# A graph network's edges ordered by source: the ordering's output written by plain DMAs to fixed rows instead of scatters

## The chip, the cores and the metric

The kernel runs on one core of one Trainium2 chip. The time is device microseconds of one execution, the median of three runs. A profile is one further execution, recorded instruction by instruction; its times below are counted from its first instruction. PE is TensorE, PEld its weight load, DVE VectorE, ACT ScalarE, POOL GpSimd, and SP SyncE, which only issues DMAs here.

## The reference

Two layers of a graph network over 20000 nodes of 256 features and 340000 edges, which come sorted by their destination `dst`:

```python
# layer 0: a relational convolution, applied twice, with relu between
xW  = einsum('ni,rio->rno', x, W)           # 8 relations
agg = segment_sum(xW[edge_type, src], dst)
h   = agg + x @ self_w + b
# x = layernorm(x + layer0)
# layer 1: attention with 4 heads, its sums taken by src
h   = (x @ W).reshape(n, 4, 64)
e   = leaky_relu(hl[src] + hr[dst]);  ee = exp(e - max over src)
out = segment_sum(ee / segment_sum(ee, src)[src] * h[dst], src)
# x = layernorm(x + layer1)
```

Layer 0 sums by destination, the order in which the edges arrive. The attention sums by source, so the edges must also be put into an order by source. This order is made on the chip, and the change is about it.

## The kernel before

Edges are taken 128 at a time, as columns of tiles with one edge on each partition: 2657 such columns ("tiles" of the rounds), 16 to a chunk, 166 chunks. Blocks are 128 nodes; there are NB = 157.

The program has four stages.

- **Start** (lines 270 to 492, driven from line 1706). `split_rows` reads x in 40 pieces and writes it as three bf16 parts to the table `xs`. Between the pieces, one step of `chunks` each prepares edge lists. After the second piece the class `ordered` (line 741) is set up and `fill_rows` writes padding rows.
- **Rounds one and two** (`round_one`, `round_two`, both through `by_chunks`, line 498). For each tile POOL gathers 128 rows of the table with an indirect DMA (`gather`, line 511), 20 tiles ahead of its use, into 24 buffers. PE multiplies the gathered parts with one-hot matrices (line 606), a chunk's sums are copied out (line 543, ACT and DVE), multiplied with the weights (line 562), and the result is written by SP. Round one writes `h2s`, which is the table of round two. Round two writes the rows of `table3s` for the attention.
- **Attention** (line 1114). For each block, 17 tiles gathered from `table3s` (line 1169) by lists loaded from `to3d`, `own3d` and `ownd`.

The order by source is made in the shadow of the rounds. `ordered.run` is a Python generator; each `yield` ends a *step*. `by_chunks` advances it with `next(side)` in those tiles for which `pace(u)` holds: in round one every tile up to number 905 and then three of four, in round two four of seven. What is left at the end of round two would run uncovered. The order of instructions on every engine is the program's order (a manual schedule), and each engine works in order, so an instruction that waits holds up what is behind it on its engine.

The generator's parts are:

- `count` (818): how many edges of each block are in each group of columns. The columns are dealt into G = 29 groups.
- `records` (793) and `places` (838): from the counts, for each group and block, the place of its first edge. A block has room for T3 = 17 columns of 128 edges, and one more that stays empty or takes an overflow; `col` is the column in which a group begins.
- `write` (895): for each group, one-hot products on PE put the edges of all blocks into place, one column for each block: a tile of 128 places by 157 blocks. What a group leaves of a column begun earlier is carried in `held`, so that a column which several groups fill is written by each of them, more complete each time. `finish` (971) transposes the tile (`turn`, 993, giving `t` with one block on each partition; two buffers) and, two steps later, `out_` (1003) writes it: for 128 and then for 29 blocks, one indirect DMA on POOL puts each block's row of 128 numbers at row `at` of `recs3`, which is block times 18 plus column. The last write to a row stands. After the last group a 30th write puts the carried rest into the next column.
- `unpack` (1062): 23 loads of 126 rows of `recs3` by SP; each is split into parts by DVE, transposed by PE, copied by ACT, and written to `ownd`, `to3d` and `own3d`.

`recs3` is set to zero at the start by 18 DMAs on ACT's queue (line 777). The scatters are lines 1006 to 1008, and `self.at` holds their row numbers, set in lines 889 to 892.

Of the kernel before, what the change touches and what calls it, by code (L numbers as in the profile page):

```python
# [34 lines left out]
F32 = mybir.dt.float32  # L35
BF16 = mybir.dt.bfloat16
I32 = mybir.dt.int32
# [3 lines left out]
ALU = mybir.AluOpType  # L41
AX = mybir.AxisListType
# [5 lines left out]
P = 128  # L48
# [8 lines left out]
T3 = 17  # L57
# [9 lines left out]
def gnn_kernel(  # L67
# [17 lines left out]
    nc = tc.nc  # L85
# [5 lines left out]
    NB = (N + P - 1) // P  # L91
# [22 lines left out]
    G = -(-COLS // GT)  # L114
# [25 lines left out]

    xp = dram.tile([NR, D], F32, name="xp")
    x1s = dram.tile([NR, D], F32, name="x1s")
    recs3 = dram.tile([NB * (T3 + 1), P], I32, name="recs3")

    ownd = dram.tile([NB * (T3 + 1), P], BF16, name="ownd")
    to3d = dram.tile([P, NB, T3 + 1], I32, name="to3d")
# [10 lines left out]
    iota = const.tile([P, P], F32, name="iota")  # L157
# [583 lines left out]
    class ordered:  # L741
# [6 lines left out]
        def __init__(self, keep, k):  # L748
            self.k = k

            self.pending = False
            self.base = keep.tile([P, 2], F32, name="base")
            nc.gpsimd.iota(self.base, pattern=[[P * (T3 + 1), 2]], base=0, channel_multiplier=T3 + 1,
                           allow_small_or_imprecise_dtypes=True)
            self.count_all = keep.tile([P, G, NB], FP16, name="count_all")
            self.place16 = keep.tile([P, NB], FP16, name="place16")
            self.cross16 = keep.tile([P, NB], FP16, name="cross16")
            self.at = keep.tile([P, 2, G + 1], I32, name="at")
            self.band = keep.tile([P, 2 * P - 1], FP16, name="band")
            nc.vector.memset(self.band, 0.0)  # L760
            nc.vector.memset(self.band[:, P - 1:P], 1.0)
            self.below = keep.tile([P, P], F32, name="below")
            nc.gpsimd.memset(self.below, 1.0)
            nc.gpsimd.affine_select(out=self.below, in_=self.below, compare_op=ALU.is_gt, fill=0.0, base=0,
                                    pattern=[[1, P]], channel_multiplier=-1)
            self.below16 = keep.tile([P, P], FP16, name="below16")
            nc.vector.tensor_copy(self.below16, self.below)
            self.ident16 = keep.tile([P, P], FP16, name="ident16")
            nc.vector.tensor_copy(self.ident16, ident)
            self.row = keep.tile([P, 1], F32, name="row")  # L770
            nc.gpsimd.iota(self.row, pattern=[[0, 1]], base=0, channel_multiplier=1,
                           allow_small_or_imprecise_dtypes=True)
            zero = keep.tile([P, NB], I32, name="zero")
            nc.vector.memset(zero, 0)
            flat = recs3.rearrange("t p -> (t p)").rearrange("(p c) -> p c", p=P)
            for c in range(T3 + 1):
                nc.scalar.dma_start(flat[:, c * NB:(c + 1) * NB], zero)

            self.lots = []
            for g in range(G):  # L780
                n = len(range(g, COLS, G))
                self.lots += [(g, i, min(LOT, n - i), n) for i in range(0, n, LOT)]
# [55 lines left out]
        def places(self, sp, ps):  # L838


            pc = ps.tile([P, 512], F32, name="pr")[:, :NB]
            for g in range(G):
                nc.tensor.matmul(pc, self.band[:, P - 1 - g:2 * P - 1 - g], self.count_all[:, g, :],
                                 start=(g == 0), stop=(g == G - 1))
            many = sp.tile([P, NB], F32, name="many", bufs=1)
            nc.scalar.copy(many, pc)
            yield
            yield
            pc = ps.tile([P, 512], F32, name="pr")[:, :NB]
            nc.tensor.matmul(pc, self.below, many, start=True, stop=True)  # L850
            begin = sp.tile([P, NB], F32, name="begin", bufs=1)
            nc.vector.tensor_copy(begin, pc)
            end = sp.tile([P, NB], F32, name="end", bufs=1)
            nc.vector.tensor_add(end, begin, many)

            over = sp.tile([P, 2, NB], F32, name="over", bufs=1)
            nc.vector.tensor_single_scalar(over[:, 0, :], many, float(P), op=ALU.is_gt)
            nc.vector.tensor_single_scalar(over[:, 1, :], end, float(T3 * P), op=ALU.is_gt)
            nc.vector.tensor_single_scalar(over[:, 1, NB - 1:], end[:, NB - 1:], float(tiles_of(NB - 1) * P), op=ALU.is_gt)
            overs = sp.tile([P, 1], F32, name="overs", bufs=1)  # L860
            nc.vector.tensor_reduce(overs, over.rearrange("p a b -> p (a b)"), op=ALU.add, axis=AX.X)
            yield
            yield
            po = ps.tile([P, 512], F32, name="pr")[:, :NB]
            nc.tensor.matmul(po[0:1, 0:1], ones[:, 0:1], overs, start=True, stop=True)
            nc.vector.tensor_add(bad, bad, po[0:1, 0:1])
            yield
            yield
            nc.vector.tensor_scalar_min(begin, begin, float(T3 * P))
            nc.vector.tensor_scalar_min(end, end, float(T3 * P))  # L870
            whole = sp.tile([P, NB], I32, name="whole", bufs=1)
            bits = sp.tile([P, NB], I32, name="bits", bufs=1)
            col = sp.tile([P, NB], F32, name="col", bufs=1)
            nc.vector.tensor_copy(whole, begin)
            nc.vector.tensor_single_scalar(bits, whole, P - 1, op=ALU.bitwise_and)
            nc.vector.tensor_copy(self.place16, bits)
            nc.vector.tensor_single_scalar(bits, whole, 7, op=ALU.arith_shift_right)
            nc.vector.tensor_copy(col, bits)
            nc.vector.tensor_copy(whole, end)
            nc.vector.tensor_single_scalar(bits, whole, 7, op=ALU.arith_shift_right)  # L880
            nc.vector.tensor_tensor(self.cross16, bits, col, op=ALU.subtract)
            nc.vector.memset(self.at, 0)
            yield
            yield
            for s in range(0, NB, P):
                n, x = min(P, NB - s), s // P
                pt = ps.tile([P, 512], F32, name="pr")
                nc.tensor.transpose(pt[:n, :P], col[:, s:s + n], ident)
                nc.vector.tensor_scalar(self.at[:n, x, :G], pt[:n, :G], self.base[:n, x:x + 1], None, op0=ALU.add)
                nxt = sp.tile([P, 1], F32, name="nxt", bufs=1)  # L890
                nc.vector.tensor_scalar(nxt[:n], pt[:n, G - 1:G], 1.0, float(T3), op0=ALU.add, op1=ALU.min)
                nc.vector.tensor_add(self.at[:n, x, G:], nxt[:n], self.base[:n, x:x + 1])
                yield

        def write(self, sp, ps, pi):
            k = self.k
# [74 lines left out]
            def finish(g, pl):  # L971
# [31 lines left out]
                def out_(c):  # L1003
                    for s in range(0, NB, P):
                        n = min(P, NB - s)
                        nc.gpsimd.indirect_dma_start(
                            out=recs3, out_offset=bass.IndirectOffsetOnAxis(ap=self.at[:n, s // P, c:c + 1], axis=0),
                            in_=v["t"][:n, s // P, :], in_offset=None)


                wait = [lambda: None] * 2
# [49 lines left out]

        def unpack(self, sp, ps):

            each = P // (T3 + 1)
            lots = [(b, min(each, NB - b)) for b in range(0, NB, each)]

            def load(b, n):
                r = sp.tile([P, 2, P], I32, name="t")[:, 0]
                nc.sync.dma_start(r[:n * (T3 + 1)], recs3[b * (T3 + 1):(b + n) * (T3 + 1), :])
                return r  # L1070

            r = load(*lots[0])
            yield
            for i, (b, n) in enumerate(lots):
                m = n * (T3 + 1)
                nxt = load(*lots[i + 1]) if i + 1 < len(lots) else None
                yield
                f = sp.tile([P, P], F32, name="uf", bufs=1)
                nc.vector.tensor_copy(f[:m], r[:m])
# [1 line left out]
                nc.vector.tensor_single_scalar(bits[:m], r[:m], P - 1, op=ALU.bitwise_and)  # L1081
                own = sp.tile([P, P], BF16, name="uo")
                nc.vector.tensor_copy(own[:m], bits[:m])
                nc.sync.dma_start(ownd[b * (T3 + 1):b * (T3 + 1) + m, :], own[:m])
                yield
                pt = ps.tile([P, 512], F32, name="pr")
                nc.tensor.transpose(pt[:, :m], f[:m], ident[:m, :m])
# [2 lines left out]
                yield  # L1090
                to = sp.tile([P, P], I32, name="ud", bufs=1)
                nc.vector.tensor_single_scalar(to[:, :m], t[:, :m], 7, op=ALU.arith_shift_right)
                nc.sync.dma_start(to3d[:, b:b + n].rearrange("p b t -> p (b t)"), to[:, :m])
                bits = sp.tile([P, P], I32, name="ub", bufs=1)
                nc.vector.tensor_single_scalar(bits[:, :m], t[:, :m], P - 1, op=ALU.bitwise_and)
                own = sp.tile([P, P], BF16, name="uo")
                nc.vector.tensor_copy(own[:, :m], bits[:, :m])
                nc.sync.dma_start(own3d[:, b:b + n].rearrange("p b t -> p (b t)"), own[:, :m])
                r = nxt

    def split(pool, v, shape, name):
# [640 lines left out]
```

## Time and profile before

| | us |
|---|---|
| median of 3 runs | 14361.06 (14348.96 to 14382.09) |
| the profiled execution | 10529.01 |
| its span, first to last instruction | 10527.3 |
| first gather of round one | 204 |
| last gather of round one, first of round two | 3612, 3635 |
| last gather of round two | 7037 |
| first scatter of the ordering, last | 1528, 6755 |
| loads of the unpacking, first and last | 6759, 6900 |
| attention's lists loaded | 7060 |

The profiled execution is 3832 us shorter than the median of the runs, and durations from the profile belong to it alone. Each stage has its own bound, so the busy share over the whole span says little; what counts is what an engine waited for within a stage. The mean granted TensorE clock was 0.968 of full speed.

### The profile page before, as it was taken

The page shows a single profiled execution, that of the slowest core. Times are in us where ns is not written, and L with a number is a line of the kernel's source. Part 1 is how long each engine was busy: PE and PEld are TensorE (multiplying, and loading weights), DVE is VectorE, ACT ScalarE, POOL GpSimd, SP SyncE. Part 2 cuts the span into 40 slices and gives each one's busy share as a digit, 9 for nine tenths or more (in the row PEclk, how much of TensorE's full clock was granted, in tenths as well). Part 3 has the DMA queues.
Part 4 walks back from the last instruction along what each step waited for, and adds up shares of the span by engine and source line. Part 5 has one row for each costly group of instructions (what it writes and reads, how often), then busy time and mean ns, then how long its engine had stood idle before and what let it go on. Part 6 is the DMA issues. An engine that isn't in the chain of part 4 may idle for free.

```text
span 10527.3 us, 226558 instructions
## 1 busy us (share of the span) xinstructions
PE 9180.0 (87%) x78961; PEld 7148.1 (68%) x78961; DVE 7514.2 (71%) x20993; ACT 5874.9 (56%) x19300; POOL 7717.9 (73%) x8094
## 2 busy tenths in 40 slices
PE   2999999999999899999999999887777777777777
PEld 2888888878888788888888888764444444444444
DVE  6666676666666666666666666438888888888888
ACT  3111145545545444444444444218888888888888
POOL 2777777777777677777777777767777777777776
PEclk6999999999999999999999999999999999999999
DMA  8666666656666566666666666665555555555554
GB/s 276 178 178 178 175 171 175 172 171 176 170 173 175 171 184 186 182 186 185 184 183 186 185 185 183 189 183 149 152 152 153 152 152 153 153 154 153 153 153 126
DMA packets 831294, 1815.05 MB, mean 172 GB/s; under 512 B 199083, under 2 KB 477820, under 8 KB 829988
## 3 DMA queue, kind: packets, MB, share of 16 engines
q0 software_dynamic: 472592, 1420.50, 49.0%
q1 hardware_dynamic: 348582, 371.97, 11.2%
q8 instruction: 620, 10.16, 0.4%
q10 hardware_dynamic: 8958, 7.99, 0.3%
q14 instruction: 542, 4.44, 0.1%
HBM read 1663.28 MB, written 136.59 MB: 171 GB/s over the span
## 4 chain that ended last, share of the span: by engine, by line
PE 52%; DVE 12%; POOL 11%; issue 10%; DMA 7%; ACT 7%; SPq 0%; ACTq 0%; DVEq 0%; POOLq 0%
PE pm L562 23%; PE a L606 15%; POOL g L1169 11%; DVE dump L1223 3%; DMA g<-table3s,to 3%; PE pl L964 3%; ACT g L1265 3%; DMA g<-xs,idx 2%; PE pm L558 2%; DVE b L788 2%; PE pr L925 1%; PE pr L728 1%; PE pr L926 1%; DMA g<-h2s,idx 1%; PE po L1279 1%
## 5 line engine op out<-in xcount | busy, mean ns | idle before, releaser
L511 POOL DMA_INDIRECT g<-xs,idx x2657 | 2525.3, 950 | 989.4 <-issue 368.3
L1169 POOL DMA_INDIRECT g<-table3s,to x2657 | 2597.9, 978 | 840.5 <-issue 775.0
L606 PE MATMUL a<-s,g 128*128 128x184 bf16 (+10 forms) x37860 | 2977.5, 223 | 204.8 <-DMA own<-xs 108.1
L511 POOL DMA_INDIRECT g<-h2s,idx x2657 | 2514.0, 946 | 826.6 <-issue 368.1
L606 PEld LDWEIGHTS <-g 128*128 128x128 bf16 x37860 | 2531.0, 98 | 549.0 <-issue 132.2
L562 PE MATMUL pm<-wt,to 128*128 128x256 f32 x10624 | 2887.7, 395 | 0.0
L1265 ACT ACTIVATE g<-g 128x64 f32<-128x64 f32 x9984 | 2435.4, 334 | 5.1
L562 PEld LDWEIGHTS pm<-wt,to 128*128 128x128 f32 x10624 | 1814.3, 191 | 177.5 <-issue 0.9
L1279 PE MATMUL po<-g,s 128*128 128x260 f32 x5314 | 1730.5, 417 | 79.7 <-DVE g L1271 50.6
L543 ACT COPY to<-a 128x512 f32<-128x512 f32 x996 | 545.5, 582 | 2242.5 <-PE a L606 2167.3
L1223 DVE CUSTOM_DVE_ANT_0 dump<-pr,pen 128x768 bf16<-128x768 f32 x1876 | 1616.6, 905 | 97.8 <-PE pr L1220 96.6
L946 DVE CUSTOM_DVE_ANT_0 dump<-pr,b 128x157 f16<-128x157 f32 x2657 | 712.3, 319 | 1105.0 <-PE pr L926 1099.0
L936 ACT ACTIVATE two<-b,hi 128x157 f16<-128x157 f16 x2657 | 1123.5, 423 | 319.7 <-DVE b L788 206.5
L1220 PE MATMUL pr<-hpt,pick 128*128 128x512 bf16 (+2 forms) x3752 | 930.5, 331 | 343.7 <-DVE top L1223 337.3
L788 DVE TENSOR_TENSOR b<-pi,kb 128x471 f16<-128x471 f32 (+1 forms) x1798 | 1109.8, 635 | 150.2 <-PE pr L830 77.5
L1279 PEld LDWEIGHTS po<-g,s 128*128 128x128 f32 x5314 | 852.2, 197 | 419.6 <-ACT g L1265 90.0
L937 ACT ACTIVATE two<-b,lo 128x157 f16<-128x157 f16 x2657 | 1101.3, 414 | 0.0
L522 DVE TENSOR_TENSOR s<-pi,code 128x1280 bf16<-128x1280 f32 (+1 forms) x666 | 1094.7, 1644 | 4.8 <-DMA xs<-s 4.8
L1220 PEld LDWEIGHTS <-pick 128*128 128x128 bf16 x3752 | 379.4, 101 | 832.8 <-issue 708.3
L1209 ACT CAST hpt<-pr 12x768 bf16<-12x768 f32 (+1 forms) x469 | 350.4, 747 | 358.9 <-PE pr L1207 358.6
L1207 PE MATMUL pr<-identb,g 128*12 128x128 bf16 x2657 | 267.2, 221 | 315.2 <-DMA g<-table3s,to 271.6
L964 PE MATMUL pl<-two,a 128*128 128x314 f16 x2657 | 509.3, 301 | 18.1 <-DVE a L952 17.2
(270 smaller groups left out, 9189.3 us busy)
## 6 DMA issues: line engine op xcount, KB each, us to landing
ob<-ownd SPq DMA_DIRECT2D x625, 128.0 KB
g<-xs,idx POOLq DMA_INDIRECT x2657
g<-h2s,idx POOLq DMA_INDIRECT x2657
g<-table3s,to POOLq DMA_INDIRECT x2657
own<-xs SPq DMA_DIRECT2D x166, 192.0 KB
h2s<-h SPq DMA_DIRECT2D x166, 192.0 KB
own<-h2s SPq DMA_DIRECT2D x166, 192.0 KB
xs<-s SPq DMA_DIRECT2D x39, 768.0 KB
```

Source lines behind the costliest of these rows:

```text
L511: nc.gpsimd.indirect_dma_start(out=g, out_offset=None, in_=table, in_offset=bass.IndirectOffsetOnAxis(ap=idx[:, u:u + 1], axis=0))
L522: nc.vector.tensor_tensor(s, pi[:, :w].unsqueeze(1).to_broadcast([P, e - f, w]), code[:, c:c + e - f].unsqueeze(2).to_broadcast([P, e - f, ...
L562: nc.tensor.matmul(p, sums[:, i % 2, i // 2, :], wt[:, i % 2, i // 2, :], start=False, stop=(i == 2 * R - 1))
L606: nc.tensor.matmul(a[h, q][:, b:e, :].rearrange("p n r -> p (n r)"), g[:, x * D + h * P:x * D + (h + 1) * P], s, start=((h, q) not in begu ...
L788: nc.vector.tensor_tensor(b[:, :n], pi[:, :NB].unsqueeze(1).to_broadcast([P, n, NB]), self.k["kb"][:, c:c + G * (n - 1) + 1:G].unsqueeze(2 ...
L936: nc.scalar.activation(two[:, 0, :], made[m][:, x, :], AF.Copy, scale=k["hi"][:, c:c + 1])
L937: nc.scalar.activation(two[:, 1, :], made[m][:, x, :], AF.Copy, scale=k["lo"][:, c:c + 1])
L1169: nc.gpsimd.indirect_dma_start(out=g[:, t, :], out_offset=None, in_=table3s, in_offset=bass.IndirectOffsetOnAxis(ap=to3[:, b, t:t + 1], ax ...
L1220: nc.tensor.matmul(pr[:, t:t + n, :], pick[:, h, :], k["hpt"][:, q + t:q + t + n, :], start=True, stop=True)
L1223: nc.vector.tensor_tensor_reduce(out=dump[:, :m, :].rearrange("p t e -> p (t e)"), in0=pr[:, :m, :].rearrange("p t e -> p (t e)"), in1=k[" ...
L1265: nc.scalar.activation(gh[:, h, :], gh[:, h, :], AF.Copy, scale=k["g"][:, t, D + h:D + h + 1])
L1279: nc.tensor.matmul(k["po"], k["s"][:, t, :] if t < n else ident, k["g"][:, t, :SR], start=(t == 0), stop=(t == n))
```

## The change

`recs3` gets a fixed row for each group and block: row 1 + group x 157 + block, 30 x 157 rows, and row 0 is all zeros. Each group's tile goes there with two plain DMAs on SP's queue instead of two scatters on POOL's; no row is written twice, and only row 0 is set to zero at the start.

Which group wrote a block's column last is now computed in `places`. For each block, with c the beginning columns of the 29 groups and the next column after the last, the number of groups whose column is at most t names the last writer of column t; it becomes a row number, or 0 if there is none. These 157 x 18 numbers go to the new tensor `cols3`, and come back into `self.at` with 128 consecutive ones in each column of `self.at`.

`unpack` then gathers, in 23 indirect DMAs on POOL of 128 rows each, the rows named by `self.at`, where SP loaded 126 consecutive rows before. Six empty steps stand before the first of them. The 23rd lot has 10 rows of use.

```diff
-    recs3 = dram.tile([NB * (T3 + 1), P], I32, name="recs3")
+    recs3 = dram.tile([(G + 1) * NB + 1, P], I32, name="recs3")
+    cols3 = dram.tile([NB * (T3 + 1), 1], I32, name="cols3")
...
-            nc.gpsimd.iota(self.base, pattern=[[P * (T3 + 1), 2]], base=0, channel_multiplier=T3 + 1,
+            nc.gpsimd.iota(self.base, pattern=[[P, 2]], base=1 - NB, channel_multiplier=1,
...
-            self.at = keep.tile([P, 2, G + 1], I32, name="at")
+            self.at = keep.tile([P, -(-NB * (T3 + 1) // P)], I32, name="at")
...
-            zero = keep.tile([P, NB], I32, name="zero")
+            zero = keep.tile([1, P], I32, name="zero")
             nc.vector.memset(zero, 0)
-            flat = recs3.rearrange("t p -> (t p)").rearrange("(p c) -> p c", p=P)
-            for c in range(T3 + 1):
-                nc.scalar.dma_start(flat[:, c * NB:(c + 1) * NB], zero)
+            nc.scalar.dma_start(recs3[0:1], zero)
...
-                nc.vector.tensor_scalar(self.at[:n, x, :G], pt[:n, :G], self.base[:n, x:x + 1], None, op0=ALU.add)
-                nxt = sp.tile([P, 1], F32, name="nxt", bufs=1)
-                nc.vector.tensor_scalar(nxt[:n], pt[:n, G - 1:G], 1.0, float(T3), op0=ALU.add, op1=ALU.min)
-                nc.vector.tensor_add(self.at[:n, x, G:], nxt[:n], self.base[:n, x:x + 1])
+                c = sp.tile([P, G + 1], F32, name="c", bufs=1)
+                nc.vector.tensor_copy(c[:n, :G], pt[:n, :G])
+                nc.vector.tensor_scalar(c[:n, G:], pt[:n, G - 1:G], 1.0, float(T3), op0=ALU.add, op1=ALU.min)
                 yield
+                upto = sp.tile([P, T3 + 1, G + 1], BF16, name="upto", bufs=1)
+                nc.vector.tensor_tensor(upto[:n], c[:n].unsqueeze(1).to_broadcast([n, T3 + 1, G + 1]),
+                                        iota[:n, :T3 + 1].unsqueeze(2).to_broadcast([n, T3 + 1, G + 1]), op=ALU.is_le)
+                w = sp.tile([P, T3 + 1], F32, name="w", bufs=1)
+                nc.vector.tensor_reduce(w[:n], upto[:n], op=ALU.add, axis=AX.X)
+                yield
+                nc.vector.tensor_scalar(w[:n], w[:n], float(NB), self.base[:n, x:x + 1], op0=ALU.mult, op1=ALU.add)
+                some = sp.tile([P, T3 + 1], F32, name="some", bufs=1)
+                nc.vector.tensor_scalar(some[:n], iota[:n, :T3 + 1], c[:n, G:], None, op0=ALU.is_le)
+                of = sp.tile([P, T3 + 1], I32, name="of", bufs=1)
+                nc.vector.tensor_mul(of[:n], w[:n], some[:n])
+                nc.sync.dma_start(cols3[s * (T3 + 1):(s + n) * (T3 + 1), :].rearrange("(p c) o -> p (c o)", p=n), of[:n])
+                yield
+            m = NB * (T3 + 1)
+            full = m // P
+            nc.sync.dma_start(self.at[:, :full], cols3[:full * P, :].rearrange("(l p) o -> p (l o)", p=P))
+            if m > full * P:
+                nc.vector.memset(self.at[:, full:], 0)
+                nc.sync.dma_start(self.at[:m - full * P, full:], cols3[full * P:, :])
+            yield
...
                 def out_(c):
                     for s in range(0, NB, P):
                         n = min(P, NB - s)
-                        nc.gpsimd.indirect_dma_start(
-                            out=recs3, out_offset=bass.IndirectOffsetOnAxis(ap=self.at[:n, s // P, c:c + 1], axis=0),
-                            in_=v["t"][:n, s // P, :], in_offset=None)
+                        nc.sync.dma_start(recs3[1 + c * NB + s:1 + c * NB + s + n, :], v["t"][:n, s // P, :])
...
-            def load(b, n):
+            def load(i):
                 r = sp.tile([P, 2, P], I32, name="t")[:, 0]
-                nc.sync.dma_start(r[:n * (T3 + 1)], recs3[b * (T3 + 1):(b + n) * (T3 + 1), :])
+                nc.gpsimd.indirect_dma_start(
+                    out=r, out_offset=None, in_=recs3,
+                    in_offset=bass.IndirectOffsetOnAxis(ap=self.at[:, i:i + 1], axis=0))
                 return r
 
-            r = load(*lots[0])
+            for _ in range(6):
+                yield
+            r = load(0)
             yield
```

The memset of `self.at` that stood ahead of the loop goes too, and the three writes of `unpack` take 128 columns of the lists at a time instead of 126.

More of the change, by code (lines that the diff above doesn't have):

```diff
@@ L881, in places @@
             nc.vector.tensor_tensor(self.cross16, bits, col, op=ALU.subtract)
-            nc.vector.memset(self.at, 0)
             yield
@@ L1062, in unpack @@
         def unpack(self, sp, ps):
-            each = P // (T3 + 1)
-            lots = [(b, min(each, NB - b)) for b in range(0, NB, each)]
-            def load(b, n):
+            of = NB * (T3 + 1)
+            lots = [(f, min(P, of - f)) for f in range(0, of, P)]
+            to3f, own3f = (t.rearrange("p b t -> p (b t)") for t in (to3d, own3d))
+            def load(i):
                 r = sp.tile([P, 2, P], I32, name="t")[:, 0]
-                nc.sync.dma_start(r[:n * (T3 + 1)], recs3[b * (T3 + 1):(b + n) * (T3 + 1), :])
-                return r
-            r = load(*lots[0])
+                nc.gpsimd.indirect_dma_start(
+                    out=r, out_offset=None, in_=recs3,
+                    in_offset=bass.IndirectOffsetOnAxis(ap=self.at[:, i:i + 1], axis=0))
+                return r
+            for _ in range(6):
+                yield
+            r = load(0)
             yield
-            for i, (b, n) in enumerate(lots):
-                m = n * (T3 + 1)
-                nxt = load(*lots[i + 1]) if i + 1 < len(lots) else None
+            for i, (b, m) in enumerate(lots):
+                nxt = load(i + 1) if i + 1 < len(lots) else None
                 yield
@@ L1083, in unpack @@
                 nc.vector.tensor_copy(own[:m], bits[:m])
-                nc.sync.dma_start(ownd[b * (T3 + 1):b * (T3 + 1) + m, :], own[:m])
+                nc.sync.dma_start(ownd[b:b + m, :], own[:m])
                 yield
@@ L1092, in unpack @@
                 nc.vector.tensor_single_scalar(to[:, :m], t[:, :m], 7, op=ALU.arith_shift_right)
-                nc.sync.dma_start(to3d[:, b:b + n].rearrange("p b t -> p (b t)"), to[:, :m])
+                nc.sync.dma_start(to3f[:, b:b + m], to[:, :m])
                 bits = sp.tile([P, P], I32, name="ub", bufs=1)
@@ L1097, in unpack @@
                 nc.vector.tensor_copy(own[:, :m], bits[:, :m])
-                nc.sync.dma_start(own3d[:, b:b + n].rearrange("p b t -> p (b t)"), own[:, :m])
+                nc.sync.dma_start(own3f[:, b:b + m], own[:, :m])
                 r = nxt
```

## The prediction

> **What bounds the kernel now.** I read the page first: busy tenths by slice, then the costliest groups. Two rounds of gathers run from 204 to about 7060 us, the attention after that.
>
> ```profile
> PE   2999999999999899999999999887777777777777
> ...
> POOL 2777777777777677777777777767777777777776
> ...
> L511 POOL DMA_INDIRECT g<-xs,idx x2657 | 2525.3, 950 | 989.4 <-issue 368.3
> ...
> L511 POOL DMA_INDIRECT g<-h2s,idx x2657 | 2514.0, 946 | 826.6 <-issue 368.1
> ```
>
> PE looks like the bound at nine tenths and POOL like an engine with a quarter free. The idle column and POOL's list of waits correct that.
>
> ```profile
> POOL g L511 <- issue: 736.4, 2417, 0.3
> POOL g L511 <- PE a L606: 468.3, 1534, 0.6
> ```
>
> The columns are total, times and longest. Nearly every gather has the same 0.30 us before it, whoever is named. So a gather costs POOL 0.95 + 0.30 = 1.25 us, and 2657 of them 3324 us of the 3408 (204 to 3612) and 3402 (3635 to 7037) that the rounds take. POOL is full in both. Next, POOL's timeline around one group's output:
>
> ```profile
> 1527.17 0.95 POOL L511 DMA_INDIRECT g<-xs,idx  x1 [0.30 <-issue]
> 1528.42 0.99 POOL L1006 DMA_INDIRECT recs<-t,at  x1 [0.31 <-issue]
> 1531.71 1.26 POOL L1006 DMA_INDIRECT recs<-t,at  x1 [2.29 <-DVE to L618]
> 1533.27 0.99 POOL L511 DMA_INDIRECT g<-xs,idx  x1 [0.30 <-PE pr L926]
> ```
>
> The second scatter stands 2.3 us after the first has been issued: both write the same tensor. From gather to gather it is 6.10 us, 4.85 over the usual 1.25. I measured all 30 pairs so: 4.7 to 7.5 us each, and 22 at the turn of the rounds, where POOL waits for h2s anyway. The 13 pairs inside round one add to 70 us, the 16 of round two to 80.
>
> Does PE feel it? Its waits between 1600 and 3550 us (first fence) and between 3700 and 6730 us (second):
>
> ```profile
> PE a L606 <- DMA g<-xs,idx: 71.1, 83, 2.8
> ```
>
> ```profile
> PE pr L720 <- ACT x L713: 31.1, 40, 1.3
> ...
> PE a L606 <- DMA g<-h2s,idx: 5.1, 9, 1.2
> ```
>
> In round one PE starves 71 us for gathers, which is the 70 us of the pairs. In round two only 5: PE is held by its own chain. I also paired the nth gather's end with the nth tile's first matmul (6 on line 606 for a tile, 12 for the middle three of a chunk). Tiles 1100 to 2600 follow by 5 us in the middle and never under 2.1, the floor of a landing. In round two the distance is 5 to 12 us, PE's pace 1.28 us a tile. At the end of the ordering the timeline shows one more stall:
>
> ```profile
> 6755.45 1.25 POOL L1006 DMA_INDIRECT recs<-t,at  x1 [2.21 <-DMA recs<-t,at]
> ...
> 6758.67 0.38 SPq L1069 DMA_DIRECT2D t<-recs  x1
> ...
> 6761.62 0.23 DVE L1079 CAST uf<-t 126x128 f32<-126x128 int32 x1 [28.92 <-DMA t<-recs]
> ...
> 6761.99 0.44 PE L1087 MATMUL pr<-ident,uf 126*128 126x126 f32 x1 [27.50 <-DVE ub L1081]
> ```
>
> The last scatters stand on POOL behind gathers issued 20 tiles ahead; the unpacking asks at once, DVE and behind it PE stand 27.5 us. POOL goes on meanwhile: right after, the distance is over 30 us. Last the start:
>
> ```profile
> 11.41 20.03 ACTq L777 DMA_DIRECT2D recs<-zero  x12
> ...
> 34.03 0.58 ACT L375 CAST lo<-pt 128x512 int32<-128x512 f32 x1 [21.58 <-DMA recs<-zero]
> ```
>
> ACT is held for 20 us by the issue of the zero writes.
>
> **What the Trainium skill says.** "Perfetto Trace Analysis", section "What 'DMA-bound' means": an issuing engine whose track is solid with DMA slices is bound by descriptor generation; the trace agrees, 1.25 us a gather with no longer gap. Its section "Identifying the Most-Contended Engine" says that matmul busy share is no measure of how near PE is to its limit; here PE is 95% busy in 1600 to 3550 (1857.06 of 1950) and still starves 71 us. "DMA: Bandwidth & Descriptors", section "Anatomy of one DMA — SWDGE (gpsimd) path": a fixed 2.0 us, most of it the receipt of the write; the second scatters' 2.2 to 2.3 us agree. "GPSIMD Engine Reference", section "Key points": indirect DMAs are possible there only, so the new gathers must go to POOL, while a plain write can go to SP.
>
> **Part by part**, against the profiled execution: 10529.0 us, span 10527.3 and 1.7 around it.
>
> *60 scatters leave POOL.* Round one: POOL is 70 us shorter, and PE's own pace there, its time less its 71 us of starving, is (1938 - 71)/1500 = 1.245 us a tile, just under POOL's 1.251. The two being nearly equal, small waits remain; I take 64 of the 70 (ends: 40, if PE's pace without starving is really 1.26, and 72). Round two: POOL is 80 us shorter, but PE at 1.28 is the limit until the ordering ends; of its starving 5 us go, up to 10 with the weight loads. POOL then runs to the limit of its 24 buffers.
>
> *60 plain writes come to SP*, about 0.34 us of issue each (that is SP's h2s and own rows), two steps after ACT made the tile, so it is there. Behind them on SP stand own rows asked for two chunks (40 us) ahead. Nothing.
>
> *The unpacking.* The 27.5 us stall goes: scatters no longer queue behind gathers, and six steps are put in, 10 tiles or 13 us against a landing of about 2. But that stall had let POOL run ahead, and the rest of the round (250 tiles, PE 1.08 to 1.22 a tile with little side work) was POOL's: it ends with the distance at 3.8 us. So what is late next is POOL, with 23 gathers more: 23 x (0.98 to 1.13 + 0.30) = 29 to 33 us. Working it out: PE reaches the old stall near 6724 instead of 6734 (in old coordinates), POOL at most 24 tiles on; 220 gathers x 1.25 + 30 = 305, end near 7030 against 7037. The unpacking steps also start 21 tiles later (11 more steps at 4 in 7), ending near tile 2555 of 2657, so they are still covered, but PE has fewer tiles to catch up in. Round two together: -6 us (ends: +15, -20).
>
> *Each new gather's waiters.* It stands on POOL behind the gather 20 tiles ahead. If POOL is at its buffers' limit it goes out when PE has freed one, about where PE is, and DVE reads it three steps (5 tiles, 6.7 us) later; landing takes 3 us from the start of a gather (0.95 + 2.1). Enough. If POOL were not ahead, DVE would wait up to 17 tiles once; PE then has POOL's pace.
>
> *Counts in DVE.* Two blocks of 18x30 compares, sums and four small operations. By rows of the trace (1280 elements of compare 1.48 us, a reduce of 432 0.60, small ones 0.16 to 0.25) some 4 us, at tile 902, where PE is 27 us behind POOL and DVE 69% busy: I take 0 (end: +4).
>
> *Columns' numbers through HBM.* Writing is 18 numbers a row. Reading back is 2816 pieces of 4 bytes: the trace has one such DMA, line 331, 166 pieces, 0.76 us of issue against 0.34, thus an estimated 7 us on SP, hidden by the 40 us ahead. 0 (end: +10).
>
> *Zero writes go at the start.* 18 DMAs, 1.45 MB, 5.2 us of all 16 engines by their packets. ACT's 20 us go, yet xs is limited by DMA afterwards (share 0.9 from 100 to 180 us). Between the two I take -10 (ends -4, -20).
>
> *Attention:* untouched, it starts earlier by the sum.
>
> Sum: -64 - 6 - 10 = -80 us, 10449 in the profile, -0.76%. The runs' median of 14361 lies 3832 above the profiled execution, and no view shows where. If that is a fixed addition, the change is -80; if all is stretched, -109. I take -94: **14267**.
>
> **Rivals.** (A) The runs without a profile are slow on POOL, so round two is POOL's as well: 150 - 30 + 10 = 130, stretched 1.364 times: 14184. For it: POOL is full in all three stages. Against: nothing shows POOL slower than 1.25. (B) They are slow on PE, POOL is always ahead, scatters and stall cost nothing: only the start, 14346. For it: PE's pace in round two. Against: a clock of 0.97. (C) Slower: the new gathers don't land in time, and each of 23 lots holds DVE, and with it PE, for w. It decides from w = 80/23 = 3.5 us; at 6 us it is +58, stretched 14440. For it: the old stall is of this kind, and DMA share there is 0.73. Against: POOL at its buffers' limit, and 6.7 us for a landing of 3.
>
> **Numbers.** Forecast 61%, A 17%, B 14%, C 8%. A measurement here can tell 0.2% (29 us) from nothing. A and nearly all of the forecast are faster by more: 0.76; B and the forecast's edge within: 0.16; C: 0.08. The forecast's own range is 14225 to 14315; to leave out two in ten it must take in part of A and B: 14170 to 14350.
>
> **What would show it.** Right: no pair gaps on POOL, 1.25 throughout; PE's 71 us of starving in round one under 20; round one shorter by 50 to 72, round two hardly; the gap before uf under 5 us; the first gather 4 to 20 us earlier. Wrong: round two shorter by over 40 (PE wasn't the limit), long gaps before uf in every lot (C), or a PE pace in round one that stays at 1.29.

## The result and the profile after

| | before | after |
|---|---|---|
| median of five runs, us | 14359.99 (14346.64 to 14382.09) | 14138.15 (14134.85 to 14161.16) |
| the profiled execution's span, us | 10527.3 | 14140.7 |

The ratio is 0.985, with a 95% interval of 0.9839 to 0.9862: the change saves 222 us, 1.5%. The forecast was 94 us, 14267, with a range of 14170 to 14350; the time lies 32 us below its end.

The two spans in the table cannot be set against each other, and this is the key to the case. Both kernels and their variants were run again later in several batches, each batch on one chip with runs of the kernel before beside it. In some batches the kernel before took 10528 to 10540 us, in others 14217 to 14377. I call these the level of 10.5 ms and the level of 14.2 ms. The profile before is from the first, the runs behind the ratio and the profile after are from the second. A chip of one number was seen at both levels, so what sets them is not known. At 14.2 the batches differ among themselves by 1%, so times at that level are compared within a batch where that is possible.

First the changed kernel's page at the level of 14.2 ms (its profile after), then that of a rerun of the same kernel at 10.5 (run after_again below). In the first two lines of each, a digit is the busy share, in tenths, of a fortieth of the span; the gathers' columns are busy us, mean ns, and idle us before them.

```profile
PE   3888888888887888888888876555555555555555
...
POOL 3666665666655555555655565444444444444443
...
L513 POOL DMA_INDIRECT g<-xs,idx x2657 | 2530.3, 952 | 1814.7 <-PE a L608 929.6
L513 POOL DMA_INDIRECT g<-h2s,idx x2657 | 2517.6, 948 | 1774.0 <-PE a L608 993.6
```

```profile
PE   3999999999999999999999999977777777777777
...
POOL 2777777777777677777777777767777777777776
...
L513 POOL DMA_INDIRECT g<-xs,idx x2657 | 2527.9, 951 | 974.8 <-issue 359.8
L513 POOL DMA_INDIRECT g<-h2s,idx x2657 | 2512.3, 946 | 878.0 <-issue 395.4
```

A gather costs POOL 0.95 us in both. What differs is the idle time before it: 1815 us against 975 in round one. At 14.2 POOL waits for PE to free buffers (the releaser named most is PE's last use of a tile); at 10.5 hardly more than the 0.3 us of its own issue stand before each gather. So PE's side is slower at 14.2, not POOL. From a gather's start to its tile's first matmul the median there is 35 us, and outside the ends of the rounds it is never under 27: POOL stands at the limit of its buffers.

The stages (first gather to last gather of each) at 14.2, from a rerun of the kernel before and the profile after, and at 10.5, from the profile before and the rerun of the changed kernel:

| us | before, 14.2 | after, 14.2 | | before, 10.5 | after, 10.5 | |
|---|---|---|---|---|---|---|
| first gather | 202.7 | 196.8 | -6 | 204.3 | 195.8 | -8.5 |
| round one | 4305.7 | 4183.2 | -122 | 3407.7 | 3341.8 | -66 |
| round two | 4359.7 | 4291.4 | -68 | 3402.0 | 3397.8 | -4 |
| attention's first gather | 8958.1 | 8758.7 | -199 | 7062.8 | 6984.0 | -79 |

At 10.5 the working of the prediction (-10, -64, -6) is met within 2 us in each stage. That is closer than batches agree: a second pair, from one batch (far_scatter, which runs as the kernel before does, and after_third), has -7, -72 and -8. At 14.2 both rounds gain much more, though POOL, whose load the change takes away, has 20 tiles to spare there. The experiments ask why.

### The profile page after: what moved, and what is told of

Its sections match the earlier page's. It is cut to its first block, busy times and chain, and to the rows that moved or that the text cites. A ratio compares the mean times of both kernels' runs of the same rounds, so it can differ in the third digit from the quotient of the medians.

```text
span 14140.7 us, 226483 instructions
## 1 busy us (share of the span) xinstructions
PE 10148.6 (72%) x78961; PEld 7702.1 (54%) x78961; DVE 7605.9 (54%) x21001; ACT 6127.3 (43%) x19300; POOL 7651.1 (54%) x8057
## 5 line engine op out<-in xcount | busy, mean ns | idle before, releaser
L608 PE MATMUL a<-s,g 128*128 128x184 bf16 (+10 forms) x37860 | 3094.5, 227 | 220.5 <-issue 108.5
L1288 ACT ACTIVATE g<-g 128x64 f32<-128x64 f32 x9984 | 2615.2, 336 | 1003.9 <-issue 984.8
L564 PE MATMUL pm<-wt,to 128*128 128x256 f32 x10624 | 2978.7, 404 | 10.0 <-issue 9.7
L608 PEld LDWEIGHTS <-g 128*128 128x128 bf16 x37860 | 2648.1, 101 | 574.3 <-issue 297.9
L1243 PE MATMUL pr<-hpt,pick 128*128 128x512 bf16 (+2 forms) x3752 | 1004.0, 354 | 2216.6 <-issue 1088.1
L1302 PE MATMUL po<-g,s 128*128 128x260 f32 x5314 | 2023.0, 479 | 94.7 <-DVE g L1294 77.9
L564 PEld LDWEIGHTS pm<-wt,to 128*128 128x128 f32 x10624 | 1872.5, 197 | 222.4 <-issue 47.6
L1302 PEld LDWEIGHTS po<-g,s 128*128 128x128 f32 x5314 | 1006.9, 229 | 518.3 <-issue 181.6
L560 PE MATMUL pm<-wt,ot 128*128 128x256 f32 x1328 | 548.0, 554 | 597.6 <-issue 386.8
L560 PEld LDWEIGHTS pm<-wt,ot 128*128 128x128 f32 x1328 | 317.4, 264 | 697.2 <-issue 429.2
```

The lines of the kernel that those rows point to most:

```text
L564: nc.tensor.matmul(p, sums[:, i % 2, i // 2, :], wt[:, i % 2, i // 2, :], start=False, stop=(i == 2 * R - 1))
L608: nc.tensor.matmul(a[h, q][:, b:e, :].rearrange("p n r -> p (n r)"), g[:, x * D + h * P:x * D + (h + 1) * P], s, start=((h, q) not in begu ...
L1243: nc.tensor.matmul(pr[:, t:t + n, :], pick[:, h, :], k["hpt"][:, q + t:q + t + n, :], start=True, stop=True)
L1288: nc.scalar.activation(gh[:, h, :], gh[:, h, :], AF.Copy, scale=k["g"][:, t, D + h:D + h + 1])
L1302: nc.tensor.matmul(k["po"], k["s"][:, t, :] if t < n else ident, k["g"][:, t, :SR], start=(t == 0), stop=(t == n))
```

## The experiments

*The two kernels once more: before_again, after_again, after_third.* No edit.

> The kernel before, unchanged, for a profile in the state of the timed runs. Theory 'the profile shown was an execution of another kind': this one takes about 14360 us with TensorE stalls that the trace puts down to no wait, as the changed kernel's does, and the attention about 5300 us. Theory 'profile and timed runs differ by the profiling': the profile is again near 10530 us.

> The changed kernel, unchanged. Two kinds of chip have been seen: one on which the kernel before takes 14360 us and TensorE is the limit of the rounds, one on which it takes 10530 and POOL is, as in the profile shown before. On the second kind the prediction's sum holds: 10530 - 80 = 10450 us, -0.76%. On the first kind it repeats 14138, -1.5%.

> The changed kernel once more, as the yardstick for the other runs beside it. Where the time before is about 10530 us: 10450 us. Where it is 14240 to 14360 us: 0.985 of it by the runs on record, 14025 us beside 14240.

before_again took 14348.27 us. after_again took 10450.12 beside 10528.01, ratio 0.9926 (0.9909 to 0.9942); after_third 10453.1 beside 10540.37, 0.9919 (0.9902 to 0.9935). So there are two levels of one program, and the profiling is not what parts them: before_again was profiled at the higher one. At the level of the profile before, the change is worth 78 and 87 us where the sum said 80. The cores' lines of the profile after and of after_again:

```profile
core 0: 14140.7 us, clock 0.846
```

```profile
core 0: 10447.8 us, clock 0.970
```

The mean granted clock differs by 13%, the time by 35%.

*What a stand of POOL costs at 10.5: pool_pause (repeated as pause_again and pause_third).* The changed kernel; at each group's write, in both halves, a copy on POOL waits for `t` as a scatter did, and four idle operations follow. No DMA is added. The two tiles that these operations write are left out of the cut.

```diff
                         nc.sync.dma_start(recs3[1 + c * NB + s:1 + c * NB + s + n, :], v["t"][:n, s // P, :])
+                        nc.gpsimd.tensor_copy(self.seen[:n], v["t"][:n, s // P, :1])
+                        for _ in range(4):
+                            nc.gpsimd.iota(self.idle, pattern=[[1, 512]], base=0, channel_multiplier=0,
+                                           allow_small_or_imprecise_dtypes=True)
```

> The changed kernel, with two stands of POOL at each group where the scatters were: a copy that waits for the same tile t, then four iotas, some 2.5 us, twice. No DMA is added. Theory 1 (what a scatter pair costs is POOL's stand and the burst of gathers after it, in which the other engines issue slowly; about 9 us a group, 29 groups): 14138 + 260 = 14400 us, at least 14300. Theory 2 (the indirect writes themselves cost): 14140 us.

> The changed kernel with the stand on POOL at each group of the copy that waits for t and four iotas, without a DMA. Where the time before is about 10530 us: 10545 us, as this kernel took there. Where it is 14240 to 14360 us: first theory: the stands are 12 to 13 us long, as the scatters' were, and cost 6 to 9 us a group, 29 groups 170 to 260 us: ratio to before 0.997 to 1.003. Second theory: as the changed kernel, 0.985.

> The changed kernel with the stand on POOL at each group of the copy that waits for t and four iotas, without a DMA, sent once more in the hope of the condition in which the kernel before takes 14240 to 14360 us. There, first theory (a group costs what POOL's stand brings with it): ratio to before 0.997 to 1.003. Second theory (the scatters' own traffic): as the changed kernel, 0.985. Where the time before is about 10530 us: 1.0015, as twice before.

Measured: 1.0014 (1.0007 to 1.0021), 1.0015 and 1.0017 of before, so all of the gain is gone; in one batch, pause_again took 103 us more than after_third. POOL's timeline of pool_pause at a group:

```profile
1528.45 0.95 POOL L513 DMA_INDIRECT g<-xs,idx  x1 [0.30 <-PE pm L552]
1529.39 0.20 POOL L1029 COPY seen<-t 128x1 int32<-128x1 int32 x1
1529.54 2.46 POOL L1031 IOTA idle<- 128x512 f32 x4
1531.95 0.17 POOL L1029 COPY seen<-t 29x1 int32<-29x1 int32 x1
1532.07 2.44 POOL L1031 IOTA idle<- 128x512 f32 x4
1534.67 0.99 POOL L513 DMA_INDIRECT g<-xs,idx  x1 [0.16 <-issue]
```

From gather to gather it is 6.22 us, where it was 6.10 with the scatters of before. The 14 to 17 us over before are about what the change adds elsewhere: 26 us for the unpacking's gathers, less 8 at the start (plain_unpack and zero_writes below). At 10.5 a scatter pair costs what it takes of POOL's time, and no further cost of it shows.

*The writes on POOL's queue: pool_plain.* The changed kernel with `nc.gpsimd.dma_start` in place of `nc.sync.dma_start` in `out_`.

> The changed kernel, its 60 writes by plain DMAs on POOL's queue: the stand for t stays (some 8 us by the trace of the kernel before), the wait for the first write's receipt goes. Theory 1: two thirds of the cost come back, 14138 + 29 x 6 = 14310 us. Theory 2 (it was the scatters' kind and their receipt): 14140 to 14170 us.

10466.81, 0.9939 (0.9922 to 0.9956): 17 us over after_again, which ran in another batch, and the intervals of the two ratios overlap. The two plain writes of a group take 1.19 us of POOL together and have no wait between them, where a pair of scatters took 4.85, 2.29 of them for the first one's receipt. It was the form of the writes, more than their queue, that cost POOL its time.

*The scatters later: late_scatter, far_scatter, far_again.* The kernel before with more empty steps ahead of `out_`: 8 in late_scatter, 26 in the other two.

```diff
-                wait = [lambda: None] * 2
+                wait = [lambda: None] * (26 if g < G - 1 else 2)
```

> The kernel before, its scatters six steps later, so that t is there when POOL comes to them; the wait for the receipt stays. Theory 1: POOL stands 5 us a group instead of 13, so a good half of the 9 us goes: 14360 - 29 x 5.5 = 14200 us. Theory 2: 14360 us.

> The kernel before with each group's scatters 24 steps later (the last group's where they were), about 50 tiles after ACT has written t, so that POOL doesn't wait for t there. The scatters and their traffic stay as they are, and so does the wait of the second scatter for the first one's receipt. Where the time before is about 10530 us: as before, 10525 to 10532 us. Where it is 14240 to 14360 us: first theory (a group costs what POOL's stand brings with it): the stand shrinks from 12 us to 5 to 7 us, a stand of 8 us costs 2.5 to 3 us a group, so 29 groups cost some 60 us in place of 220: ratio to before 0.988 to 0.991. Second theory (it is the scatters' own traffic): ratio 1.0.

> The kernel before with each group's scatters 24 steps later (the last group's where they were), so that POOL doesn't wait for t, with the same traffic. Where the time before is 14240 to 14360 us: first theory (POOL's stand): ratio to before 0.988 to 0.991. Second theory (the scatters' own traffic): 1.0. Where it is about 10530 us: 1.0.

The ratios were 1.0 (0.9991 to 1.0009), 1.0 (0.9991 to 1.0008), both at 10.5, and at 14.2 1.0003 (0.9994 to 1.0012). They tell nothing of either theory, because the edit moved nothing. In all traces the first scatters stand behind the 1048th gather, then the 1172nd, the 1296th and so on. The reason is in `bring`: a group's first lot starts with `while later: one()`, which issues what is left of the list, and that is one lot (three steps) after the list was made. The steps of `wait` are therefore empty for every group but the last, also in the kernel before. POOL's waits show that the stand for `t` in far_again is that of before_again; first before_again, then far_again (us in total, times, longest):

```profile
POOL recs L1006 <- ACT t L1001: 153.6, 26, 9.1
```

```profile
POOL recs L1006 <- ACT t L1001: 159.9, 25, 9.2
```

*The stall before the unpacking: six_steps.* The kernel before with the six empty steps that the change puts ahead of the first load.

> The kernel before with the six empty steps ahead of its unpacking, nothing else. If the stall of 27.5 us of the first profile were part of the timed runs: 14330 us. If POOL is at its buffers' limit in the timed runs, the stall isn't there: 14360 us, within 15.

10531.72, 1.0003 (0.9994 to 1.0011). The first cast's wait fell from 28.92 us to

```profile
6763.65 0.23 DVE L1081 CAST uf<-t 126x128 f32<-126x128 int32 x1 [10.43 <-DMA t<-recs]
```

and the time stayed. POOL ends the round at 10.5, and what DVE and PE no longer stand there is given back later.

*The unpacking's gathers: plain_unpack.* The changed kernel with plain loads of consecutive rows in the unpacking; they are not the rows that are wanted, so the attention works on other edges.

```diff
-                nc.gpsimd.indirect_dma_start(
-                    out=r, out_offset=None, in_=recs3,
-                    in_offset=bass.IndirectOffsetOnAxis(ap=self.at[:, i:i + 1], axis=0))
+                nc.sync.dma_start(r, recs3[i * P:(i + 1) * P, :])
```

> The changed kernel, but the unpacking loads 128 consecutive rows by SP instead of gathering rows on POOL (other rows than the reference's, so other edges in the attention). Where POOL is the limit, the 23 gathers cost 23 x 1.28 = 29 us of round two: 29 us under after_again. Where TensorE is the limit, the trace of the changed kernel shows a pace of 1.77 us a tile in the 150 tiles of the unpacking against 1.55 before: 33 us under it.

10424.19, 0.9898 (0.9881 to 0.9914), 26 us under after_again in the same batch (28 in round two's stage): the price of the 23 gathers.

*The zero writes: zero_writes.* The changed kernel with the 18 DMAs of zeros put back, into a tensor that nothing reads.

```diff
...
+            flat = spare.rearrange("t p -> (t p)").rearrange("(p c) -> p c", p=P)
+            for c in range(T3 + 1):
+                nc.scalar.dma_start(flat[:, c * NB:(c + 1) * NB], zero)
```

> The changed kernel with the 18 zero writes at the start again, into a tensor that nobody reads. By the prediction the start's part is 10 us: 10 us over after_again, between 4 and 20; by the traces of the two chips (first gather at 204.3 and 202.7 before, 196.8 after) 6 to 8.

10458.13, 0.9932 (0.9916 to 0.9949), 8 us over after_again in the same batch.

*A stand at 14.2: pool_wait, pool_long, pause_fourth.* All three are the changed kernel with a stand at each group and no DMA in it: pool_wait the copy that waits for `t` alone, pool_long with `range(12)` in the edit of pool_pause, pause_fourth as pool_pause. Each of a group's two halves gets them, so that a group has 24 idle operations in pool_long (13.4 us) and not twelve, as its expectation says.

> After, with one copy on POOL at each group that reads one element of the lot's t, so that POOL stands there until ACT has written it, and no DMA. Nothing that is computed changes. Where the time before is about 10530 us (POOL limits): the copy takes some 0.35 us of POOL at each of 60 groups, 20 us, so 10455 to 10465 us by either theory. Where it is about 14360 us (TensorE limits): first theory (what a scatter pair costs there is POOL's stand for t, after which the gathers go out back to back): 29 groups with 6 to 9 us each, 14310 to 14360 us. Second theory (it is the scatters' own transfers): as after, 14140 us.

> After, with a stand on POOL at each group of the copy that waits for t and twelve iotas, about 7 us of work behind it; no DMA. Where the time before is about 10530 us: four iotas cost 95 us over after, so twelve cost about 3 times that less what the first ones had hidden: 10720 to 10800 us. Where it is about 14360 us: first theory: at least 29 groups with 9 us, 14400 us or more, since a longer stand makes a longer burst. Second theory: POOL's slack of 20 tiles hides it, 14140 us.

> The changed kernel with the stand of the copy that waits for t and four iotas at each group, sent for the condition in which the kernel before takes 14240 to 14360 us. There, first theory (POOL's stand): ratio to before 0.997 to 1.003. Second theory (the scatters' own traffic): 0.985, as the changed kernel. Where the time before is about 10530 us: 1.0016.

pool_wait: 14131.11 beside 14237.05, 0.9919 (0.9903 to 0.9936). The 14140 us of the second theory were meant for a kernel before of 14360; beside 14237 the ratio tells, and it lies between the 0.985 of the change and 1. pool_long: 1.0176 (1.0159 to 1.0193). pause_fourth: 14231.75 beside 14217.46, 1.0014 (0.9999 to 1.0028). So stands of POOL without any scatter take back the whole gain here too, and the second theory, that the scatters' own transfers cost the time, is not needed: without them it is as slow. What each stand costs, from tile 900 to 2600 of round one (13 groups); the yardstick is two_lists (below), which is the changed kernel up to the attention and ran in the batch of pool_wait and pool_long:

| | gather to gather over the group, us | PE from tile 900 to 2600, us | more than without, for a group |
|---|---|---|---|
| two_lists | 2.0 | 2674.2 | |
| pool_wait | 7.7 | 2713.3 | 3.0 |
| pool_long | 21.8 | 2882.1 | 16.0 |
| the profile after | 1.9 | 2701.5 | |
| before_again | 12.2 | 2815.4 | 8.8 |
| pause_fourth | 12.1 | 2775.4 | no yardstick in its batch |
| far_again (the scatters of before) | 12.8 | 2792.1 | no yardstick in its batch |

The 3.0 us of pool_wait are half of the 6 to 9 that the first theory expected, and its stand is shorter than that of the scatters, 7.7 us against 12.2. For a stand of 12.2 us the line between the two without scatters gives 3.0 + 4.5/14.1 x 13.0 = 7.1, and the scatters' cost 8.8; the yardsticks of the two figures, from two batches, differ by 27 us in 13 groups, 2 for each. In one batch, pause_fourth and far_again differ by 17 us in these 13 groups, 1.3 for each, at stands of 12.1 and 12.8 us, and in round two (tiles 2800 to 5080) by 4.5 us in 14, 0.3 for each. So nearly all of what a pair costs comes with the stand; up to two us may be the scatters' own, or the difference between batches.

Why does PE lose, if it has 20 tiles in its buffers? Busy times in stretches before, in and behind one stand; first pool_long (the stand is 4144 to 4165), then before_again (a scatter pair, 4105 to 4117):

```profile
core 0: us, PE busy (x) PEld busy (x) DVE busy (x) ACT busy (x) POOL busy (x), PEclk, DMA share, GB/s
4122.00:4142.00 20.00, 16.66 (x155) 13.78 (x154) 10.90 (x34) 6.77 (x20) 12.47 (x14) 0.91 0.52 149
4146.00:4166.00 20.00, 17.82 (x164) 15.19 (x162) 14.38 (x45) 8.85 (x27) 14.48 (x27) 0.91 0.09 29
4170.00:4190.00 20.00, 5.17 (x34) 2.83 (x33) 0.92 (x3) 0.63 (x2) 15.21 (x16) 0.67 0.63 177
```

```profile
4083.00:4103.00 20.00, 16.72 (x169) 14.24 (x166) 12.62 (x39) 7.87 (x24) 12.51 (x14) 0.96 0.51 146
4105.00:4117.00 12.00, 11.90 (x114) 10.11 (x112) 7.63 (x28) 3.85 (x12) 2.99 (x3) 1.00 0.12 35
4117.00:4137.00 20.00, 7.88 (x74) 6.04 (x72) 8.16 (x25) 6.53 (x21) 13.48 (x15) 0.71 0.51 144
```

While POOL stands and hardly a gather goes out, PE is not late at all: it is busier than before, 17.82 of 20 us. The time is lost behind the stand. POOL then has many free buffers and sends its gathers without a gap, 16 in 20 us, and PE falls to 34 matmuls in 20 us. It doesn't starve: the tiles that it works on were gathered 20 us before and more. PE's waits in pool_long from 4164 to 4185 us are put down to nothing that the trace shows:

```profile
PEld L608 <- issue: 7.2, 7, 1.3
PE a L608 <- issue: 6.2, 7, 1.8
...
PEld L552 <- issue: 5.1, 4, 1.9
PE pm L552 <- issue: 4.3, 5, 1.2
```

From 4172 us on PE starts its instructions at distances of about 0.7 us or a multiple of it. DVE and ACT stand as well. POOL begins the burst's last gather at 4189.01 and then stands for 3.76 us; at 4193.3 to 4193.4 all three engines go on, DVE after 22.45 us and ACT after 22.80.

Now the same density of gathers at 10.5, in the profile before:

```profile
2400.00:2420.00 20.00, 19.92 (x196) 16.79 (x196) 14.31 (x47) 10.66 (x32) 15.12 (x17) 1.00 0.66 189
```

17 gathers in 20 us, a DMA share of 0.66, and PE is full.

The rounds as a whole agree. I sorted the time from 1400 us to shortly before the unpacking by how many gathers POOL had begun in the last 10 us, and took gaps of over 0.3 us between matmuls as PE's idle time. In before_again PE is idle for 11% at 6 gathers, 27% at 7 and 62% at 8; in the profile before for 4% at 8, where that kernel is nearly all the time. So gathers without a gap slow the other engines at 14.2 and not at 10.5. At 14.2, then, a stand of POOL costs through the burst that it sets off behind it. The fetching of instructions shows no sign of being the cause: its 620 packets of 16 KB take 0.99 us each in the middle at both levels.

The granted clock drops too, to 0.67. The Trainium skill ("TensorE: Matmul & The Clock Gate", Part 1) says that the default state of PE's clock is the throttled one and that activity releases it; the stretches agree, 0.91 to 1.00 where PE is busy and 0.67 to 0.71 where it stands. By that, part of the low mean clock of 0.846 follows from the standing and is not its cause; how much the runs don't say.

*Fewer packets for the attention's lists: wide_lists, two_lists.* The changed kernel with a block's list in one DMA (wide_lists), or in two (two_lists, shown), in place of five.

```diff
-                n = min(4, tiles_of(b) - 4 * q)
+                n = min(9, tiles_of(b) - 9 * q)
...
-                at = b * (T3 + 1) + 4 * q
+                at = b * (T3 + 1) + 9 * q
...
```

> The changed kernel with the attention's list of a block loaded by one DMA of 4352 bytes a partition instead of five of at most 1024: a quarter of the packets, the same bytes. Theory A (on the chip of 14360 us the engines issue slowly after bursts of DMA packets[...]): 157 x 1000 packets less, 1 to 2 ms less there. Theory B (it is the gathers' bursts alone): no change there. On the other kind of chip, no change by more than 30 us by either.

> After, with attention's list of a lot read by two DMAs of up to nine tiles (up to 2304 bytes a partition) in place of five of four tiles: the same bytes in fewer packets. Where the time before is about 10530 us: no change, 10447 to 10452 us. Where it is about 14360 us: if bursts of packets are what slows attention's steps, over half of the slow part of each step goes, some 5 us in each of 150 steps, 13400 us; if not, 14138 us.

At 10.5, wide_lists: 10446.65, 0.9923 (0.9906 to 0.9939), no change against after_again. At 14.2, two_lists: 13992.55, 0.9819 (0.9802 to 0.9835). Its attention takes 5234 us from the first gather to the last, against 5287 and 5284 in pool_wait and pool_long of the same batch. That is 50 us, not the 700 or so of the expectation: packets of the lists are a small part of what slows the engines there, and what the rest is stays open. It is the fastest version measured at 14.2; the changed kernel itself wasn't in that batch, and against its ratio of 0.985 the intervals just part.

## Why the prediction was right and wrong

Right, at the level of its profile, step by step, with the rerun after_again against the profile before:

- *Scatters leave POOL, round one, -64:* -66. The pair gaps are gone. In the window from 1600 to 3550 us PE starves for gathers

```profile
PE a L608 <- DMA g<-xs,idx: 10.5, 15, 2.3
```

  where it was 71.1, and the bound of "under 20" held.
- *Plain writes on SP, 0:* right in size, but the working said that `t` is there when they are issued. It isn't: SP waits for it in 29 groups, 234 us in all, and its write begins 0.03 us after ACT's copy ends, since the two waiting steps never act but in the last group (see late_scatter). What hid it was named: the rows behind it on SP are wanted 40 us later.
- *Unpacking, -6 in round two:* -4. That the stall was cover for POOL, and its removal worth nothing by itself, is shown by six_steps; the 29 to 33 us for the gathers were 26. "Enough" was wrong for their landing: DVE's cast waits for one in 17 of 23 lots, 2.69 us in the first, 5.06 at most and 54.3 in all, and PE stands 28.9 us for these casts and the operation behind them. This is what rival C described, at 54.3/23 = 2.4 us a lot, under the 3.5 from which it decides. By the trace it costs nothing here, since POOL ends the round: at tile 5295 PE again follows its gather by 3.1 us. At 14.2 no wait of a cast is put down to these gathers.
- *Start, -10:* -8.5 in the trace, 8 by zero_writes. *Counts, columns through HBM, attention, 0 each:* nothing is left over, since the stages add to -79 and the medians to -78 (-87 in the other batch).

Wrong: *the step from the profile to the runs*, "a fixed addition" or "all is stretched", between which -94 was taken. The 3832 us were neither. At 14.2 the time is not the profile's plus or times something: another engine sets it, and each term of the sum changes for itself. Start -6 (for -10), round one -122 (for -64), round two -68 (for -6), the rest -9: -206 in the traces, -222 in the medians. The two terms that were mis-sized are those of the scatters, and each was taken from POOL's time or PE's starving in the profile. Of round one's 122 us, 114 lie between tiles 900 and 2600, where its 13 groups are (8.8 each, where the working had 5); in round two, from tile 2800 to 5080, 14 groups take 97 us longer before than after (7 each, where the working had next to nothing), and the unpacking gives 33 back (tiles 5100 to 5250, 1.77 us a tile against 1.55; why it costs this at 14.2, no run shows).

Of the rivals, A was nearest in time (14184), but by luck, since its mechanism was wrong: POOL's gather is 0.95 us at both levels. B had the premise right, "slow on PE, POOL is always ahead", and its conclusion wrong, that scatters then "cost nothing". Its counter-evidence, a clock of 0.97, was taken from the very execution that didn't have the level of the runs.

Open is what the level is: what makes it, and through what a burst of gathers holds PE, ACT and DVE. That the burst follows from POOL's stand, and not from the scatters' transfers, is shown by pause_fourth. That the scatters' transfers add nothing was meant to be shown by far_again, and wasn't: up to two us a group are left for them.

## What to carry to other kernels

Where the profiled execution and the runs differ by much more than the change can bring (here 3832 us against 80), the profile shows another regime: work out each part for both possible bounds, and don't scale the sum. An engine that is far ahead doesn't make its stands free: ask what it does when it is released, and whether the burst behind the stand hits something shared. And before a step is called "two steps later", follow the list that issues it to the place where it is emptied.

## What was not expected of the hardware

- One program takes 10528 or 14360 us, 36% apart, in different batches of runs, with POOL's gather at 0.95 us in both. A packet of POOL's queue takes as long as well, 166 ns in the middle.
- At 14.2, 16 gathers in 20 us left PE 5.17 us of work; at 10.5, 17 in 20 us left it 19.92. In the stretch at 14.2 PE started its instructions about every 0.7 us or a multiple of it, and PE, DVE and ACT went on together some 4 us after the burst's last gather had begun.
- At 14.2 a stand of POOL of 12 us costs 7 to 9 us of PE's time in round one, though some 20 tiles lie ready for PE when it begins.
